# A graph-attention layer with residual and layer norm: rows led by their own column taken from SBUF instead of gathered

## The chip, the cores and the metric

The kernel runs on one core of one Trainium2 chip. The metric is the device time of one execution in microseconds (us). Before the change it was 237.32 us, the median of three runs (237.05 to 239.15).

Engine names are those of the profile: PE is TensorE (PEld its weight loads), DVE is VectorE, ACT is ScalarE, POOL is GpSimd, SP is the engine that issues most DMAs. A trailing q (SPq) stands for an engine's sequencer.

## The reference, cut to what matters

The inputs are x (4096 x 512), adj (4096 x 4096), W (512 x 2048, four heads of 512) and a (the attention vectors), all float32.

```
ht    = (x @ W) per head                                 # 4 heads, 4096 x 512
e     = leaky_relu(src[i] + dst[j], 0.01) + adj[i, j]    # src, dst: ht times a
att   = softmax(e over j)
h     = mean over heads of (att @ ht)
out   = layernorm(x + h)                                 # eps 1e-5, no gain
```

adj is not a mask here: its entries are 0 where there is no edge and otherwise random weights of up to 1e9, and the diagonal always has an edge. In a row whose largest entry stands far enough above the rest, the softmax puts all its weight on that one column c. Then h[i] = x[c] @ (mean of W over the heads), and the output row is layernorm(x[i] + x[c] @ W_mean).

## The kernel before, in words

`leading_rows` computes this short form for all rows and, beside it, a test that the leading entry is far enough ahead in every row. If a row fails the test, `general` computes its block in full; otherwise it is passed over.

**Tiling.** The 4096 rows are cut into NB = 32 blocks of 128. Partition p of block ib holds row p * 32 + ib. `hold` is one SBUF tile [128, 32, 512] for x of all blocks; at first its slots 16 to 31 hold W, and at the end each slot holds the block's output. `adj_t` has six buffers of 2 MB, one block each.

**The loop.** One step t of the loop (L408 on) works on several blocks at once:

- SP asks for four blocks of x where `x_at` says so (L403, L411), and for the adj tile of block t + 5 (L413). The first x load, for blocks 0 to 3, is asked for ahead of the loop (L132), behind the first five adj tiles and W.
- DVE reduces the adj tile of block t to the maxima of 64 segments of 64 columns, in two halves (`segment_maxima`, L163). Between the halves stands `find_column` of block t - 2 (L194): `max` and `max_index` in the 64 values of the leading segment, which a gather has fetched.
- POOL, for block t - 2, adds the segment's start to the place within the segment (L200) and gathers the 128 rows of x (`gather_rows`, L186) into `y`. In even steps it then computes the reciprocal deviation of two older blocks (`rstd`, L255 to L257).
- DVE finds the leading segment of block t (`find_segment`, L170 to L172). POOL turns it into a row of `adj_segs` (L174), gathers the segments (`lead`, L176), and multiplies the segment number by 64 (`start`, L181).
- PE, for block t - 3, transposes y (`turn`, L213; ACT copies the result, L215), adds the residual x by a product with the identity (`residual`, L221), and multiplies by the mean of W (`products`, L228). In the first steps it also transposes W and forms the vectors of the test (L334, L342).
- ACT takes the sums for the norm of block t - 4 (`stats`, L250, L252) and of x (`row_norm`, L235), and writes the finished blocks (`finish`, L261).

**Late blocks.** BEHIND is 24. For blocks 24 to 31 x is loaded only at the end; the products are put by and x is added later (`put_by`, `add_x`). The last block finds its column in the whole row (`find_column_in_row`). The stores follow the loop on SP (`store`, L313).

**What sets the order.** The kernel runs under a manual schedule: every engine executes its instructions in the order in which the Python code issues them. An engine that waits holds up all that is behind it in its own order. `small` tiles have five buffers each, `y` has four.

Of the kernel before, what the change touches and what calls it, by code (L numbers as in the profile page):

```python
# [9 lines left out]
F32 = mybir.dt.float32  # L10
U32 = mybir.dt.uint32
I32 = mybir.dt.int32
AF = mybir.ActivationFunctionType
OP = mybir.AluOpType
# [6 lines left out]
P = 128  # L21
C = 512
E = 64
# [3 lines left out]
def gat_resnorm_kernel(  # L27
# [29 lines left out]
    any_bad = keep.tile([1, 1], I32, name="any_bad")  # L57

    leading_rows(tc, x, adj, W, a, out, ident, v, n_bad, any_bad)

    flag = nc.values_load(any_bad[0:1, 0:1], min_val=0, max_val=N)
# [5 lines left out]
def leading_rows(ctx, tc, x, adj, W, a, out, ident, v, n_bad, any_bad):  # L67
# [8 lines left out]
    nc = tc.nc  # L76
    N, D = x.shape
    H = a.shape[0]
    KB, NB, S = D // P, N // P, N // E
    AHEAD = 5  # L80
    Q = 4
    PIECES = 4
    LATE = NB - Q
    BEHIND = LATE - Q

    once = ctx.enter_context(tc.tile_pool(name="once", bufs=1))
    adj_pool = ctx.enter_context(tc.tile_pool(name="adj_pool", bufs=AHEAD + 1))
    y_pool = ctx.enter_context(tc.tile_pool(name="y_pool", bufs=4))
    lead_pool = ctx.enter_context(tc.tile_pool(name="lead_pool", bufs=2 * Q + 1))
    small = ctx.enter_context(tc.tile_pool(name="small", bufs=5))  # L90
# [11 lines left out]
    hold = once.tile([P, NB, D], F32, name="hold")  # L102
# [1 line left out]
    w_sum = once.tile([P, KB, D], F32, name="w_sum")  # L104
    a_rows = once.tile([2 * H, D], F32, name="a_rows")

    once.tile([P, 32], F32, name="pad_end")
    adj_t = {}

    def pieces(ib):  # L110
# [30 lines left out]
    width = once.tile([P, 1], U32, name="width")  # L141
    nc.gpsimd.iota(width, pattern=[[0, 1]], base=E, channel_multiplier=0)
    power = once.tile([P, 2], F32, name="power")
    nc.gpsimd.memset(power, -0.5)
    eps = once.tile([P, 1], F32, name="eps")
    nc.gpsimd.memset(eps, EPS)

# [7 lines left out]
    seg_of, at_of, lead_of, y_t, yt_of, o_ps = {}, {}, {}, {}, {}, {}  # L155
# [12 lines left out]
    def find_segment(ib):  # L168
        seg = seg_of.pop(ib)
        nc.vector.max(out=top[:, ib, :], in_=seg)  # L170
        at = small.tile([P, 8], U32, name="at")
        nc.vector.max_index(at, top[:, ib, :], seg)  # L172
        row = small.tile([P, 1], U32, name="row")
        nc.gpsimd.tensor_tensor(row, at[:, 0:1], first[:, ib : ib + 1], op=OP.add)  # L174
        lead = lead_pool.tile([P, E], F32, name="lead")
        nc.gpsimd.indirect_dma_start(  # L176
            out=lead, out_offset=None, in_=adj_segs,
            in_offset=bass.IndirectOffsetOnAxis(ap=row[:, :1], axis=0),
        )
        start = at_of[ib] = small.tile([P, 1], U32, name="start")  # L180
        nc.gpsimd.tensor_tensor(start, at[:, 0:1], width, op=OP.mult)  # L181
        lead_of[ib] = lead

    def gather_rows(ib, col):
        y = y_t[ib] = y_pool.tile([P, D], F32, name="y")
        nc.gpsimd.indirect_dma_start(  # L186
            out=y, out_offset=None, in_=x,
            in_offset=bass.IndirectOffsetOnAxis(ap=col[:, :1], axis=0),
        )

    def find_inner(ib):
        nc.vector.max(out=inner[:, ib, :], in_=lead_of[ib])

    def find_column(ib):  # L194
        if ib < BEHIND:
            find_inner(ib)
        within = small.tile([P, 8], U32, name="within")
        nc.vector.max_index(within, top[:, ib, :], lead_of[ib])  # L198
        col = small.tile([P, 1], U32, name="col")
        nc.gpsimd.tensor_tensor(col, at_of.pop(ib), within[:, 0:1], op=OP.add)  # L200
        gather_rows(ib, col)

    def find_column_in_row(ib):

        col = small.tile([P, 8], U32, name="col")
        nc.vector.max_index(col, top[:, ib, :], adj_t[ib])
        gather_rows(ib, col)
# [192 lines left out]
        nc.vector.tensor_reduce(total, pg, axis=AX.X, op=OP.add)  # L400
        nc.vector.tensor_scalar(any_bad, total, -1.0, float(N), op0=OP.mult, op1=OP.add)

    x_at = {lo - 1: (lo, Q) for lo in range(Q, BEHIND, Q)}  # L403
    vectors = [(kb, h) for kb in range(KB) for h in range(H)]
    vectors_at = {t: 2 if t < 3 else 1 for t in range(1, 15)}
    COLUMN, PROJECT, STATS, FINISH = 2, 3, 4, 6
# [1 line left out]
    for t in range(NB):  # L408
# [7 lines left out]
        if t >= COLUMN:  # L416
            find_column(t - COLUMN)
# [4 lines left out]
        if t == NB - 1:  # L422
            for ib, n in ((BEHIND, 2), (LATE, Q), (BEHIND + 2, 2)):
                load_x(ib, n)
        find_segment(t)
        if t < 2:
            mean_of_heads(t)
# [8 lines left out]
        ib = t - PROJECT  # L436
# [23 lines left out]
    for ib in range(2 * Q, BEHIND, 2):  # L460
        store(nc.sync, ib, 2)
    find_column(NB - 2)
    add_x(nc.gpsimd, BEHIND)
    add_x(nc.gpsimd, BEHIND + 1)
# [211 lines left out]
```

## Time and profile before

| | |
|---|---|
| median of three runs | 237.32 us |
| span of the profiled execution | 235.7 us |
| DVE busy | 186.6 us (79%) |
| PE busy | 195.5 us (83%) |
| POOL busy | 100.9 us (43%) |
| ACT busy | 111.8 us (47%) |
| moved by DMA | 97.73 MB, mean 415 GB/s |
| gather of x rows (y), issue to landing, median | 7.7 us |
| gather of segments (lead), issue to landing, median | 6.1 us |
| adj tile of 2 MB, issue to landing, median | 31.8 us |

The profile is of one execution, whose span runs from its first to its last instruction; its time by the clock of the other runs isn't given apart from that, and the median stands 1.6 us above the span. A line of the timeline gives start and duration in us, engine, line of the kernel, operation, output tile and input tiles, with shapes, and in brackets how long the engine stood idle before it and what ended that. A line of a tile's view gives shortest/median/longest duration in ns, and the first and last start. The DMA row gives, for 40 equal slices of the span, the busy share in tenths (9 is 90% or more). A line of a queue gives packets, MB and the share of the 16 DMA engines' time.

### The profile page before, as it was taken

Reading aid. Unit: us, or ns where it says so; the run is one execution under the profiler, and the core shown is the slowest. Engines: PE = TensorE matmul, PEld = TensorE weight load, DVE = VectorE, ACT = ScalarE, POOL = GpSimd, SP = SyncE. Lnnn points to the kernel's source line nnn. Section 1 sums busy time; section 2 is a strip of 40 time slices with the busy share of each in tenths; the row PEclk is TensorE's granted clock in tenths of the full one; section 3 lists DMA queues with packets and bytes.
Section 4 is the critical chain, followed back from the end, with each engine's and each line's share of the span. In section 5 each row is a group of like instructions: output and inputs, shape, how many; then the busy total and the mean of one; then the engine's idle time right before and its main releaser. Section 6 shows DMA issues by size and latency. Waiting matters only on the chain.

```text
span 235.7 us, 2500 instructions
## 1 busy us (share of the span) xinstructions
PE 195.5 (83%) x683; PEld 100.9 (43%) x683; DVE 186.6 (79%) x302; ACT 111.8 (47%) x267; POOL 100.9 (43%) x215
## 2 busy tenths in 40 slices
PE   0198959999999899999969879688787987799991
PEld 0034526456555565665424333243333432245460
DVE  1735884589959995999589979998699899989772
ACT  2012012155757547474748355546464554137782
POOL 1112232415526462646353654464365564549130
PEclk9999799999999999999999999999997999999998
DMA  6999999999999999999999999999999999999995
GB/s 226 441 432 417 446 414 439 415 436 415 435 429 418 428 427 443 425 419 434 425 428 434 423 434 423 432 416 432 426 436 415 422 427 417 421 425 418 416 360 212
DMA packets 13697, 97.73 MB, mean 415 GB/s; under 512 B 2152, under 2 KB 2152, under 8 KB 7792
## 3 DMA queue, kind: packets, MB, share of 16 engines
q1 hardware_dynamic: 10080, 88.08, 88.5%
q0 software_dynamic: 3584, 9.44, 10.1%
q8 instruction: 6, 0.10, 0.2%
q14 instruction: 11, 0.09, 0.1%
q10 hardware_dynamic: 16, 0.02, 0.0%
HBM read 89.15 MB, written 8.39 MB: 414 GB/s over the span
## 4 chain that ended last, share of the span: by engine, by line
issue 33%; POOL 33%; DMA 18%; PE 9%; DVE 3%; POOLq 1%; ACT 1%; SPq 1%
DMA adj_t<-in_adj_dram 15%; POOL lead L176 11%; POOL y L186 10%; PE o L228 5%; POOL sd L256 4%; DMA y<-in_x_dram,col 3%; POOL start L181 2%; POOL col L200 2%; POOL row L174 2%; DVE seg L163 2%; PE o L270 2%; POOL sd L255 1%; POOL nm L257 1%; PE tp L213 1%; PE o L221 1%
## 5 line engine op out<-in xcount | busy, mean ns | idle before, releaser
L163 DVE TENSOR_REDUCE seg<-adj_t 128x32 f32<-128x2048 f32 (+1 forms) x68 | 145.9, 2150 | 35.3 <-DMA adj_t<-in_adj_dram 34.6
L228 PE MATMUL o<-w_sum,yt 128*128 128x512 f32 x248 | 116.5, 610 | 1.0 <-ACT yt L215 1.0
L228 PEld LDWEIGHTS o<-w_sum,yt 128*128 128x128 f32 x248 | 44.7, 193 | 54.9 <-issue 42.5
L215 ACT COPY yt<-tp 128x512 f32<-128x512 f32 x32 | 18.8, 588 | 47.3 <-PE tp L213 47.3
L176 POOL DMA_INDIRECT lead<-in_adj_dram,row x32 | 32.2, 1008 | 14.3 <-POOL row L174 14.3
L186 POOL DMA_INDIRECT y<-in_x_dram,col x32 | 30.8, 962 | 15.9 <-POOL col L200 15.6
L213 PE MATMUL tp<-ident,y 128*128 128x128 f32 x128 | 19.6, 276 | 15.0 <-DMA y<-in_x_dram,col 14.7
L318 PE MATMUL o<-hold,ident 128*128 128x512 f32 x32 | 18.6, 733 | 15.5 <-DMA hold<-in_L_gnn_W_dram 15.5
L221 PE MATMUL o<-hold,ident 128*128 128x512 f32 x52 | 26.9, 598 | 0.5 <-DMA hold<-in_x_dram 0.5
L213 PEld LDWEIGHTS tp<-ident,y 128*128 128x128 f32 x128 | 14.5, 141 | 28.2 <-issue 26.7
L200 POOL TENSOR_TENSOR col<-start,within 128x1 uint32<-128x1 uint32 x31 | 5.8, 188 | 45.7 <-DVE within L198 45.7
L336 ACT COPY wt<-tp 128x512 f32<-128x512 f32 x16 | 9.2, 587 | 32.4 <-PE tp L334 32.4
L174 POOL TENSOR_TENSOR row<-at,first 128x1 uint32<-128x1 uint32 x32 | 6.0, 188 | 39.3 <-DVE at L172 39.3
L235 ACT ACTIVATE sq<-hold 128x512 f32<-128x512 f32 x32 | 19.8, 620 | 0.0
L342 PEld LDWEIGHTS pv<-at_d,wt 128*128 128x128 f32 x128 | 16.3, 191 | 6.8 <-ACT wt L336 3.5
L318 PEld LDWEIGHTS o<-hold,ident 128*128 128x128 f32 x32 | 7.2, 237 | 24.6 <-POOL row L174 11.1
L319 ACT ACTIVATE w_sum<-o 128x512 f32<-128x512 f32 x4 | 2.4, 598 | 31.5 <-PE o L318 31.5
L261 ACT ACTIVATE hold<-o,nm,sd 128x512 f32<-128x512 f32 x24 | 17.2, 771 | 0.0
L252 ACT ACTIVATE sq<-o,nm 128x512 f32<-128x512 f32 x24 | 16.5, 687 | 0.8
L342 PE MATMUL pv<-at_d,wt 128*128 128x2 f32 x128 | 15.3, 244 | 0.6 <-ACT wt L336 0.6
L250 ACT ACTIVATE sq<-o 128x512 f32<-128x512 f32 x24 | 14.6, 607 | 0.0
L334 PEld LDWEIGHTS tp<-ident,hold 128*128 128x128 f32 x64 | 7.9, 142 | 6.9 <-issue 6.9
(85 smaller groups left out, 137.2 us busy)
## 6 DMA issues: line engine op xcount, KB each, us to landing
adj_t<-in_adj_dram SPq DMA_DIRECT2D x27, 2048.0 KB, 31.8
hold<-in_x_dram SPq DMA_DIRECT2D x7, 1024.0 KB, 32.6
adj_t<-in_adj_dram SPq DMA_DIRECT2D x6, 1024.0 KB, 28.3
out_dram<-hold SPq DMA_DIRECT2D x10, 512.0 KB, 15.0
adj_t<-in_adj_dram SPq DMA_DIRECT2D x8, 512.0 KB, 6.2
hold<-in_L_gnn_W_dram SPq DMA_DIRECT2D x4, 1024.0 KB, 17.3
out_dram<-hold SPq DMA_DIRECT2D x2, 1024.0 KB, 15.7
hold<-in_x_dram SPq DMA_DIRECT2D x2, 512.0 KB, 14.9
```

What stands on the lines that cost most here:

```text
L163: nc.vector.tensor_reduce(seg_of[ib][:, ts(k, S // n)], adj_t[ib][:, ts(k, N // n)].rearrange("p (s e) -> p s e", e=E), axis=AX.X, op=OP.max,)
L176: nc.gpsimd.indirect_dma_start(out=lead, out_offset=None, in_=adj_segs, in_offset=bass.IndirectOffsetOnAxis(ap=row[:, :1], axis=0),)
L186: nc.gpsimd.indirect_dma_start(out=y, out_offset=None, in_=x, in_offset=bass.IndirectOffsetOnAxis(ap=col[:, :1], axis=0),)
L213: nc.tensor.transpose(tp[:, kb, :], y[:, ts(kb, P)], ident)
L215: nc.scalar.copy(yt, tp)
L221: nc.tensor.matmul(o_ps[ib], ident, hold[:, ib, :], start=start, stop=False)
L228: nc.tensor.matmul(o_ps[ib], yt_of[ib][:, kb, :], w_sum[:, kb, :], start=(start and kb == 0), stop=(kb == KB - 1),)
L235: nc.scalar.activation(sq, hold[:, ib, :], AF.Square, accum_out=xx[:, ib : ib + 1])
L252: nc.scalar.activation(sq, o, AF.Square, bias=nm[:, i], accum_out=sd[:, i])
L261: nc.scalar.activation(hold[:, ib, :], o_ps.pop(ib), AF.Identity, bias=nm[:, i], scale=sd[:, i])
L318: nc.tensor.matmul(o, ident, hold[:, w_at + kb * H + h, :], start=(h == 0), stop=(h == H - 1))
L342: nc.tensor.matmul(pv[:, kb, h : 2 * H : H], wt[:, k, :], at_d[:, k, h : 2 * H : H], start=(k == 0), stop=(k == KB - 1),)
```

## The change

For blocks 0 to 23, rows whose leading column is their own row number are treated apart. The column is formed in float32 (`col_f`, from `start_f`, which replaces the integer `start`), compared with the row number (`own`, a new tile made by an iota), and 4096 is added to the index of the rows that are equal (`row_or_none`). y is first written by POOL as x of the block times the result of the comparison (`here`): x in the rows led by themselves, 0 elsewhere. Then the gather is issued with a bound of 4095, so that indices above it are passed over and those rows of y keep what POOL wrote. Blocks 24 to 31 keep the old path. The loads of x in the loop are asked for at step lo - 2 instead of lo - 1 for blocks lo to lo + 3. A padding tile is larger.

```diff
-    once.tile([P, 32], F32, name="pad_end")
+    once.tile([P, 128], F32, name="pad_end")
...
+    own = once.tile([P, NB], F32, name="own")
+    nc.gpsimd.iota(
+        own, pattern=[[1, NB]], base=0, channel_multiplier=NB, allow_small_or_imprecise_dtypes=True
+    )
...
-        start = at_of[ib] = small.tile([P, 1], U32, name="start")
-        nc.gpsimd.tensor_tensor(start, at[:, 0:1], width, op=OP.mult)
+        if ib < BEHIND:
+            start = small.tile([P, 1], F32, name="start_f")
+            nc.gpsimd.tensor_scalar(start, at[:, 0:1], float(E), None, op0=OP.mult)
+        else:
+            start = small.tile([P, 1], U32, name="start")
+            nc.gpsimd.tensor_tensor(start, at[:, 0:1], width, op=OP.mult)
+        at_of[ib] = start
...
+    def gather_others(ib, start, within):
+
+        col = small.tile([P, 1], F32, name="col_f")
+        nc.gpsimd.tensor_scalar(col, within, start, None, op0=OP.add)
+        here = small.tile([P, 1], F32, name="here")
+        nc.gpsimd.tensor_scalar(here, col, own[:, ib : ib + 1], None, op0=OP.is_equal)
+        row = small.tile([P, 1], U32, name="row_or_none")
+        nc.gpsimd.tensor_scalar(row, here, float(N), col, op0=OP.mult, op1=OP.add)
+        y = y_t[ib] = y_pool.tile([P, D], F32, name="y")
+        nc.gpsimd.tensor_scalar(y, hold[:, ib, :], here, None, op0=OP.mult)
+        nc.gpsimd.indirect_dma_start(
+            out=y, out_offset=None, in_=x,
+            in_offset=bass.IndirectOffsetOnAxis(ap=row[:, :1], axis=0),
+            bounds_check=N - 1, oob_is_err=False,
+        )
...
+        if ib < BEHIND:
+            gather_others(ib, at_of.pop(ib), within[:, 0:1])
+            return
...
-    x_at = {lo - 1: (lo, Q) for lo in range(Q, BEHIND, Q)}
+    x_at = {lo - 2: (lo, Q) for lo in range(Q, BEHIND, Q)}
```

## The prediction

> **What bounds the kernel now.** I read the page first (engine shares, DMA row, queues), then the engines' timelines around the waits, and last the chain.
>
> ```profile
> PE 195.5 (83%) x683; PEld 100.9 (43%) x683; DVE 186.6 (79%) x302; ACT 111.8 (47%) x267; POOL 100.9 (43%) x215
> DMA  6999999999999999999999999999999999999995
> q1 hardware_dynamic: 10080, 88.08, 88.5%
> q0 software_dynamic: 3584, 9.44, 10.1%
> ```
>
> The DMA row stands at nine tenths or more in 38 of 40 slices: the transfers are the resource with no slack, and no engine is full over the whole span. q0 carries POOL's gathers, 9.44 MB: 32 gathers of 128 x rows of 2 KB (8.39 MB) and 32 of 128 segments of 256 B. So bytes not gathered are DMA time, up to where something else takes over. VectorE's timeline tells where that is:
>
> ```profile
> 158.58 2.29 DVE L163 TENSOR_REDUCE seg<-adj_t 128x32 f32<-128x2048 f32 x1 [0.25 <-DMA adj_t<-in_adj_dram]
> 166.82 2.29 DVE L163 TENSOR_REDUCE seg<-adj_t 128x32 f32<-128x2048 f32 x1 [2.78 <-DMA adj_t<-in_adj_dram]
> 183.50 2.29 DVE L163 TENSOR_REDUCE seg<-adj_t 128x32 f32<-128x2048 f32 x1 [0.43 <-DMA adj_t<-in_adj_dram]
> 206.04 0.09 DVE L198 MATCH_VALUE_LOAD within<-top,lead 128x8 f32 x1 [0.39 <-DMA lead<-in_adj_dram,row]
> ```
>
> The bracket is idle time and its releaser. The wait at 166.8 (step 24) is the last long one for an adj tile; it comes once in four steps, behind each x load. From there VectorE runs its own steps back to back until the last tile is reduced at 209.7, then TensorE's chain of products runs to the last store. The end can move forward only as far as step 24 does. Steps are told by `within` (L198): done at 41.5 in step 4, 56.2 in 6, 105.8 in 14, 169.4 in 24, 180.2 in 26.
>
> Now POOL, over two steps:
>
> ```profile
> 103.77 0.96 POOL L176 DMA_INDIRECT lead<-in_adj_dram,row  x1 [0.51 <-POOL row L174]
> 104.75 0.20 POOL L181 TENSOR_TENSOR start<-at,width 128x1 uint32<-128x1 uint32 x1
> 105.91 0.19 POOL L200 TENSOR_TENSOR col<-start,within 128x1 uint32<-128x1 uint32 x1 [0.96 <-DVE within L198]
> 106.64 0.96 POOL L186 DMA_INDIRECT y<-in_x_dram,col  x1 [0.54 <-POOL col L200]
> 107.68 0.19 POOL L255 TENSOR_SCALAR sd<-sd 128x2 f32<-128x2 f32 x1
> 107.95 0.72 POOL L256 TENSOR_TENSOR sd<-sd,power 128x2 f32<-128x2 f32 x1
> 108.75 0.20 POOL L257 TENSOR_TENSOR nm<-nm,sd 128x2 f32<-128x2 f32 x1
> 108.90 0.19 POOL L174 TENSOR_TENSOR row<-at,first 128x1 uint32<-128x1 uint32 x1
> 109.47 1.06 POOL L176 DMA_INDIRECT lead<-in_adj_dram,row  x1 [0.38 <-POOL row L174]
> 110.57 0.21 POOL L181 TENSOR_TENSOR start<-at,width 128x1 uint32<-128x1 uint32 x1
> 111.49 0.19 POOL L200 TENSOR_TENSOR col<-start,within 128x1 uint32<-128x1 uint32 x1 [0.71 <-DVE within L198]
> ```
>
> POOL looks idle at 43%, but in an even step (with the three rstd operations) it waits only 0.7 us for VectorE. Without waits for other engines the even step costs it 4.9 us (105.91 to 110.78) and the odd one 3.6, together about 8.4, against 12.58 us for which two steps last (169.4 - 56.2, over nine pairs). It is in order: what is put ahead of the `lead` gather delays VectorE two steps later. Last, the start:
>
> ```profile
> 36.56 0.96 POOL L176 DMA_INDIRECT lead<-in_adj_dram,row  x1 [0.27 <-POOL row L174]
> 42.12 1.12 PE L221 MATMUL o<-hold,ident 128*128 128x512 f32 x2 [0.55 <-DMA hold<-in_x_dram]
> L244 POOL TENSOR_TENSOR hold<-hold,adj_t x3: 1273/1279/1283, 213.7 to 217.4; 128x512 f32<-128x512 f32 x3
> ```
>
> The first x load (blocks 0 to 3) lands only at 42.1, when TensorE waits for it, while POOL gathers y of block 0 already at 26.4. The last line is the only POOL operation on a 128x512 tile: 1.28 us with two inputs.
>
> **What the Trainium skill says.** GPSIMD Engine Reference, section "Elementwise — side-by-side cycle accounting": about 2.6 cycles an element at 1.2 GHz with two inputs (512 elements, 1.11 us, plus dispatch), and for a tight loop 769 ns measured on 512 elements. The trace agrees on the first (1.28 us); it shows nothing with one wide input. DMA: Bandwidth & Descriptors, section "Queues, rings and completion order": each DMA engine takes turns between the queues that have work, so gather bytes left out are turns for the adj stream. The trace fits: gathers land in 6.1 and 7.7 us while an adj tile needs 31.8. No page bears on what an index out of bounds costs.
>
> **The change, part by part.**
>
> *Rows skipped.* Counted in the reference's own inputs, 240 of the 3072 rows of blocks 0 to 23 have their maximum on the diagonal. 240 x 2048 B = 0.49 MB, at 427 GB/s (the rate of the middle windows) 1.15 us. Only the 204 rows of blocks 0 to 20 are gathered in time to move the tile of step 24: 0.98 us. That is the ceiling of the gain at the end.
>
> *Small operations.* `col` (0.19) becomes col_f, here and row_or_none, three dependent ones of 0.27 each start to start (as L255 to L256), and start_f stands for start. Unshown: whether compare and scalar forms cost more; L255, a TENSOR_SCALAR, costs 0.19, so I take that.
>
> *The wide multiply* y = hold x here. Unshown. Below: ident's TENSOR_SCALAR_AFFINE_SELECT on 128x128 took 0.29 us, so four times the width at least 0.5. Above: 1.28 us (L244). I take 0.8, the skill's 512-element price. The gather then waits 0.54 us for y as it did for col. So `within` to y gather grows from 0.73 to 0.81 + 0.80 + 0.54 = 2.15 us, +1.42 per block, bounds +1.1 to +1.9; 24 blocks are 34 us of POOL. The check of bounds I take at nothing, with 0 to 0.25 us per gather kept for the range.
>
> *What that does to the cadence.* Every even step's `lead` needs the one two steps before. The loop: 0.08 handshake, 2.15, y gather 1.04, rstd 1.23, row 0.57, landing of lead 6.1, `within` 0.5: 11.7 us. POOL itself needs 5.0 + 6.25 = 11.25 for both steps. Until step 14 TensorE's turns of W hold a pair at 12.12 (turns at 97.65, 103.71, 109.77). All are under 12.58, so the addition hides under the DMA stream, with under 1 us to spare per pair.
>
> *The new wait for x.* Block 0's multiply reads hold and waits for the first x load; behind it in POOL's queue stand y of block 0, lead of 2, y of 1, lead of 3. These four, 0.59 MB, no longer precede the load, so it lands 1.4 us sooner, at 40.7. Then multiply to 41.5, y gather 42.0, row 43.1, lead of block 2 43.6 (was 29.2), landed 49.7, `within` in step 4 at 50.2 instead of 41.5: VectorE is 8.7 us late, TensorE's first block likewise. Does DMA run dry? No: four to five adj tiles are in flight (31.8 us from issue to landing). Recovery: steps 5 and 6 go at VectorE's own 5.55, 11.1 where they took 14.7: 5.0 late at step 6. Four pairs to step 14 at 12.12 against 12.41 (105.8 - 56.2): 3.8 late. Five pairs to step 24 at 11.7 (58.5) against 63.6 give back 5.1: all made up, by little, so step 24 is DMA-bound again, 0.9 sooner. From 24 to 26 VectorE took 10.8; the loop needs 11.7 less 0.2 (no L192), so `within` comes at 168.5 + 11.5 = 180.0 against 180.2. After that blocks take the old path.
>
> *x two steps ahead.* The bytes stay; each x load passes one adj load on SP, so the gap behind it comes a step earlier (7, 11, ... 23). It lands one step before its multiply. SP waits no longer for it: nothing. The larger pad and `own`: nothing; one more iota at the start hides before 10.5, when POOL first has work.
>
> *Sum:* -0.2 us against the profiled span, 235.5 for 235.7; the median of the runs, 237.32, has 1.6 us around that, taken as unchanged: 237.1.
>
> **The rivals.**
> *POOL paces the loop (slower).* If multiply plus check cost 1.28 us, POOL needs 5.5 + 6.7 = 12.2 for two steps: the delay of 5.4 at step 6 shrinks by only 9 x 0.37 = 3.3, and steps 24 to 26 take 12.2 instead of 10.8: +3.3, 240.6. At 1.5 us it is 12.65, nothing is recovered: +8, 245. It decides from about 1.05 us. For it: 1.28 is the only wide POOL row, and the descriptor work with bounds isn't shown; against: one input, not two.
> *The skip moves no bytes less* (an index out of bounds still takes its turn): the recovery still holds, the ceiling is gone: +0.5, 237.8. Against it only that a row not written must not be fetched.
> *Cheap POOL (0.5 us):* the loop is 11.4 and the end takes most of the ceiling: -0.8, 236.5; I count it with the forecast.
>
> **The numbers.** A measurement of this kernel tells about 1% (2.4 us) from no change. Forecast with the cheap case 0.60; POOL pacing 0.27, nearly all over +1%; no bytes saved 0.08; 0.05 for what I don't see, mostly a gain over the ceiling. Low end 235.9: ceiling plus 0.3% noise; high end 241.5: pacing at 1.33 us, which leaves out 0.11 above and 0.04 below.
>
> **What would show it.** POOL's busy time rising from 101 to about 135 us; the multiply near 0.8 us; y of block 0 gathered near 42 instead of 26; `within` waiting for lead in steps 4 to 6; q0 at about 8.95 MB; a wait for an adj tile at step 23 still there, near 161. If that wait is gone and `within` waits for lead in most even steps, POOL paces. If POOL's first multiply starts near 27, the first x load isn't the wait I take it for. It is all wrong if y's landing, not lead's, turns out to hold the steps.

## The result, and the profile after

The changed kernel takes 255.32 us, the median of four runs (254.58 to 257.74), against 238.02 for the kernel before in the runs beside it. The ratio is 1.074, with an interval of 1.066 to 1.081: 17 us slower. The profiled execution has a span of 252.9 us, 17.2 more than before.

The page of the changed kernel, its engine shares, the DMA row and the queue of the gathers:

```profile
PE 201.0 (79%) x683; PEld 103.8 (41%) x683; DVE 186.4 (74%) x302; ACT 112.1 (44%) x267; POOL 159.9 (63%) x288
DMA  6999999999999999999999999999999999972215
q0 software_dynamic: 3584, 8.95, 9.4%
```

The change does what it says: q0 moved 8.95 MB for 9.44. But POOL is busy for 59 us more, and DMA, full to the end before, has little to do in the last four slices. The loads run ahead and the engines come behind. Who waits for whom (columns: total us, times, longest), first the kernel before, then the changed one:

```profile
DVE seg L163 <- DMA adj_t<-in_adj_dram: 34.6, 14, 5.5
DVE within L198 <- DMA lead<-in_adj_dram,row: 1.0, 2, 0.6
```

```profile
DVE inner L217 <- DMA lead<-in_adj_dram,row: 33.6, 17, 10.9
POOL row L178 <- DVE at L176: 22.5, 6, 8.6
DVE seg L167 <- DMA adj_t<-in_adj_dram: 16.9, 6, 5.5
POOL y L209 <- DMA hold<-in_x_dram: 13.5, 1, 13.5
```

VectorE used to wait for adj tiles, now it waits for the `lead` gathers. Its last wait for an adj tile is at 38.2; before it was at 183.5. The sum of VectorE's work is unchanged (186.4 us).

POOL over two steps of the changed kernel, from its timeline:

```profile
100.29 0.29 POOL L203 TENSOR_SCALAR col_f<-within,start_f 128x1 f32<-128x1 uint32 x1
100.68 0.29 POOL L205 TENSOR_SCALAR here<-col_f,own 128x1 f32<-128x1 f32 x1
101.08 0.27 POOL L207 TENSOR_SCALAR row_or_none<-here,col_f 128x1 uint32<-128x1 f32 x1
101.45 1.58 POOL L209 TENSOR_SCALAR y<-hold,here 128x512 f32<-128x512 f32 x1
103.31 1.11 POOL L210 DMA_INDIRECT y<-in_x_dram,row_or_none  x1 [0.28 <-POOL y L209]
...
106.15 0.30 POOL L203 TENSOR_SCALAR col_f<-within,start_f 128x1 f32<-128x1 uint32 x1
...
113.48 0.29 POOL L203 TENSOR_SCALAR col_f<-within,start_f 128x1 f32<-128x1 uint32 x1
```

POOL waits for no other engine here, in the lines left out neither. The two steps last 13.19 us (100.29 to 113.48), all of it POOL's own work and the gaps between its dependent operations. Before, two steps lasted 12.58 on the mean of nine pairs; in the changed kernel the same nine pairs last 13.31. From the first operation to the start of the y gather it is 3.02 us instead of 0.73.

The end of `within` (L198 before, L223 in the changed kernel) in some steps, in us of each profiled execution, and how far the changed kernel is behind:

| step | before | changed | behind |
|---|---|---|---|
| 4 | 41.5 | 51.8 | 10.3 |
| 6 | 56.2 | 65.2 | 9.0 |
| 14 | 105.8 | 118.9 | 13.1 |
| 24 | 169.4 | 185.0 | 15.5 |
| 28 | 191.2 | 209.7 | 18.5 |
| last (block 30) | 211.3 | 228.9 | 17.6 |

So the loss has two parts: some 9 us at the start, and a slower pace that adds 6.5 from step 6 to 24. Two or three more come between steps 24 and 28, where VectorE waits for `lead` three times, 3.2 us in all, while POOL works off blocks 22 and 23.

### The profile page after: what moved, and what is told of

The parts are those of the page before. It is cut to its first block, busy times and chain, and to the rows that moved or that the text cites. A ratio compares the mean times of both kernels' runs of the same rounds, so it can differ in the third digit from the quotient of the medians.

```text
span 252.9 us, 2596 instructions
## 1 busy us (share of the span) xinstructions
PE 201.0 (79%) x683; PEld 103.8 (41%) x683; DVE 186.4 (74%) x302; ACT 112.1 (44%) x267; POOL 159.9 (63%) x288
## 3 DMA queue, kind: packets, MB, share of 16 engines
q0 software_dynamic: 3584, 8.95, 9.4%
## 4 chain that ended last, share of the span: by engine, by line
POOL 42%; DMA 21%; issue 17%; PE 16%; DVE 2%; ACT 1%; POOLq 0%
POOL y L209 12%; PE o L256 9%; DMA adj_t<-in_adj_dram 9%; POOL y L210 8%; POOL lead L180 8%; DMA lead<-in_adj_dram,row 6%; DMA y<-in_x_dram,row_or_none 3%; POOL sd L284 3%; DMA y<-in_x_dram,col 3%; POOL here L205 2%; POOL col_f L203 2%; PE o L249 2%; PE tp L241 2%; POOL row L178 2%; POOL start_f L186 1%
## 5 line engine op out<-in xcount | busy, mean ns | idle before, releaser
L256 PE MATMUL o<-w_sum,yt 128*128 128x512 f32 x248 | 117.7, 616 | 1.0 <-ACT yt L243 1.0
L256 PEld LDWEIGHTS o<-w_sum,yt 128*128 128x128 f32 x248 | 45.5, 195 | 56.1 <-issue 43.7
L209 POOL TENSOR_SCALAR y<-hold,here 128x512 f32<-128x512 f32 x24 | 38.0, 1582 | 15.6 <-DMA hold<-in_x_dram 13.5
L241 PE MATMUL tp<-ident,y 128*128 128x128 f32 x128 | 20.6, 286 | 29.1 <-DMA y<-in_x_dram,row_or_none 25.8
L346 PE MATMUL o<-hold,ident 128*128 128x512 f32 x32 | 19.4, 761 | 15.9 <-DMA hold<-in_L_gnn_W_dram 15.9
L217 DVE MAX8 inner<-lead 128x8 f32<-128x64 f32 x32 | 6.5, 221 | 33.7 <-DMA lead<-in_adj_dram,row 33.6
L210 POOL DMA_INDIRECT y<-in_x_dram,row_or_none x24 | 26.6, 1106 | 6.7 <-POOL y L209 6.7
L249 PE MATMUL o<-hold,ident 128*128 128x512 f32 x52 | 28.4, 630 | 0.0
L370 PEld LDWEIGHTS pv<-at_d,wt 128*128 128x128 f32 x128 | 17.2, 200 | 7.4 <-issue 4.1
L289 ACT ACTIVATE hold<-o,nm,sd 128x512 f32<-128x512 f32 x24 | 17.2, 771 | 0.0
L370 PE MATMUL pv<-at_d,wt 128*128 128x2 f32 x128 | 16.0, 249 | 0.6 <-ACT wt L364 0.6
```

Source lines behind the costliest of these rows:

```text
L209: nc.gpsimd.tensor_scalar(y, hold[:, ib, :], here, None, op0=OP.mult)
L210: nc.gpsimd.indirect_dma_start(out=y, out_offset=None, in_=x, in_offset=bass.IndirectOffsetOnAxis(ap=row[:, :1], axis=0), bounds_check=N - ...
L241: nc.tensor.transpose(tp[:, kb, :], y[:, ts(kb, P)], ident)
L249: nc.tensor.matmul(o_ps[ib], ident, hold[:, ib, :], start=start, stop=False)
L256: nc.tensor.matmul(o_ps[ib], yt_of[ib][:, kb, :], w_sum[:, kb, :], start=(start and kb == 0), stop=(kb == KB - 1),)
L289: nc.scalar.activation(hold[:, ib, :], o_ps.pop(ib), AF.Identity, bias=nm[:, i], scale=sd[:, i])
```

## The experiments

Two theories stood against each other at first: POOL's pace makes the loss by itself, or the stall at the start is a loss of its own. A third suspect was the order of the loads. Ratios are to runs of the kernel before on the same chip, with the 95% interval.

### The x loads alone

```diff
 # the kernel before
-    x_at = {lo - 1: (lo, Q) for lo in range(Q, BEHIND, Q)}
+    x_at = {lo - 2: (lo, Q) for lo in range(Q, BEHIND, Q)}
```

> The kernel before with one part of the change alone: the x loads of the loop asked for at step lo - 2 instead of lo - 1. Theory (POOL's added work and its wait for the first x load make the 17 us): same as before, 238 us within 1 us, waits for an adj tile move from steps 8, 12, ... to 7, 11, ... Rival (the order of the loads matters by itself, x passing an adj tile delays VectorE): 2 us or more slower than before.

Measured: 237.16 us, ratio 0.999 (0.9965 to 1.001). `within` is 2.9 to 3.0 us behind in steps 7, 11 and 15 and 0.5 or less in the step after each. VectorE's wait moves by one step, as expected, and costs nothing. The order of the loads by itself is out.

### Pace without stall

```diff
 # the changed kernel, at both places
-        if ib < BEHIND:
+        if Q <= ib < BEHIND:
```

> The changed kernel, with blocks 0 to 3 on the old path (gathered in full, no multiply), so that POOL never waits for the first x load. Theory (the stall of 13.5 us at the start costs about 9 us, and POOL's pair of steps of 13.2 us never pays it back): about 246 us, within 2; within of step 6 within 1 us of before, POOL still full from about step 8 on. Rival (POOL's pace alone makes the whole loss, the stall is hidden behind it as a slack that would be used up anyway): 252 us or more.

Measured: 247.55 us, ratio 1.038 (1.030 to 1.046), as expected. Step 6 is 1.1 us behind the kernel before, step 24 8.4, step 28 10.7; the nine pairs of steps between 6 and 24 last 13.4 us on the mean. (The profiled execution was 1.4 us behind already at step 2, before anything of the change acts, and so was that of the next run.) The slower pace alone costs about 10 us, and it costs it with no stall ahead.

### Stall without pace

```diff
 # the changed kernel, at both places
-        if ib < BEHIND:
+        if ib < Q:
```

> The new path for blocks 0 to 3 alone, the old one for 4 to 23: the stall of POOL at the start stays, the slower pace goes. Theory (stall and pace only cost together: with the old pace of 8.4 us of POOL for two steps the delay of some 9 us at step 6 is paid back by step 24 out of the 14 us in which VectorE waits for adj tiles): within 1 us of before. Rival (a stall at the start is a loss of its own that stays): 243 us or more.

Measured: 240.94 us, ratio 1.012 (1.006 to 1.018), between the two expectations. Step 6 is 10.3 us behind, step 24 3.5, the end 2 to 4. The delay is paid back for two thirds, not in full: a pair lasted 11.8 us. Two waits of the trace stand in the way. POOL's rstd waits for ScalarE's sums, which come behind TensorE, and behind step 16 VectorE waits 2.46 us for a product of the test, which also comes late from TensorE (0.56 us in the kernel before):

```profile
105.40 0.19 POOL L283 TENSOR_SCALAR sd<-sd 128x2 f32<-128x2 f32 x1 [1.84 <-ACT sq L280]
117.52 0.19 POOL L283 TENSOR_SCALAR sd<-sd 128x2 f32<-128x2 f32 x1 [2.25 <-ACT sq L280]
131.59 0.19 DVE L382 TENSOR_REDUCE n<-px 128x8 f32<-128x32 f32 x1 [2.46 <-PE px L380]
```

How much each of the two waits costs was not tried apart.

The profiled spans are longer by 4.1 us with the stall alone, by 10.2 with the pace alone, by 17.2 with both. The two together cost about 3 us more than their sum (3.7 by the medians, 3.6, 10.0 and 17.3). That fits a POOL that is full, so that the stall has nothing from which to be paid back. Neither of the two theories was right alone.

### The wide operation left out

```diff
 # blocks 0 to 3 on the old path, and
-        nc.gpsimd.tensor_scalar(y, hold[:, ib, :], here, None, op0=OP.mult)
```

> Blocks 0 to 3 on the old path, and the multiply left out in the others: the rows led by themselves are skipped by the gather and y keeps an older block's row there, so this part of the computation is missing. No engine writes y but the gather. Theory (the multiply of 1.58 us, not the small operations or the gather with bounds, makes POOL the pace, and the run with ScalarE failed because the copy stood at the end of ScalarE's step): POOL's pair falls from 13.2 to about 9.5 us, 236.5 to 238 us. Rival (the longer way from within to the gather costs by itself): 240 us or more.

Measured: 236.94 us, ratio 0.998 (0.995 to 1.001). POOL waits for VectorE again, and VectorE hardly for `lead`:

```profile
POOL col_f L203 <- DVE within L222: 16.5, 20, 2.0
DVE inner L216 <- DMA lead<-in_adj_dram,row: 3.9, 5, 0.9
```

The small operations and the gather with bounds are still there (0.29, 0.29, 0.27 and 1.12 us). So with them in place and without the stall, the wide operation makes the whole difference to the run with the slower pace, 247.55 us; a run with it and without the small operations was not made. Step 24 ends 0.8 us ahead of before; from step 26 on that is gone, with VectorE waiting 0.6 and 0.7 us for `lead` in steps 25 and 26.

### Half the width

```diff
 # the changed kernel
-        nc.gpsimd.tensor_scalar(y, hold[:, ib, :], here, None, op0=OP.mult)
+        n = D if ib < Q else D // 2
+        nc.gpsimd.tensor_scalar(y[:, :n], hold[:, ib, :n], here, None, op0=OP.mult)
```

> The changed kernel with the multiply on half of the columns in blocks 4 to 23 (in the other half the rows led by themselves keep older values: that part is left out). The wide operation should take about 0.9 us, near the 0.8 of the prediction. By the prediction's recurrence: the early delay is paid back, 237.5 to 239 us. By the corrected one (small operations 0.40 apart instead of 0.27, gather 1.10 instead of 0.96, so a loop of 12.3 us for two steps against 12.58): only some 3 of 9 us are paid back by step 24, 243 to 246 us.

Measured: 247.94 us, ratio 1.047 (1.042 to 1.051). The operation took 0.94 us, close to the price of the prediction, and still nothing was paid back: 8.8 us behind at step 6, 10.2 at step 24. A pair lasted 12.7 us, more than both recurrences gave, and both expectations missed. So even near the price that I had assumed, the step "all made up" fails.

POOL's own work for two steps was at most 12.2 us (103.5 to 115.7), so something else is longest. The trace shows hardly any landing times, but a wait of VectorE for `lead` ends with the landing. In five of the six odd steps from 13 to 23 it waited, and there `lead` had been issued 7.4 to 9.2 us before. For block 13:

```profile
114.22 0.97 POOL L180 DMA_INDIRECT lead<-in_adj_dram,row  x1 [0.28 <-POOL row L178]
122.90 0.23 DVE L218 MAX8 inner<-lead 128x8 f32<-128x64 f32 x1 [2.25 <-DMA lead<-in_adj_dram,row]
```

From the end of `within` in step 13 (110.1) to that in step 15 (123.3) it is 13.2 us: 4.1 to the issue of `lead`, 8.7 to its landing, 0.4 for VectorE. The way through `lead` in the odd steps, which the prediction's recurrence doesn't contain, is the longest here. It is read from the trace; no run changes it alone.

### All rows fetched

```diff
 # the changed kernel
-        nc.gpsimd.tensor_scalar(row, here, float(N), col, op0=OP.mult, op1=OP.add)
+        nc.gpsimd.tensor_scalar(row, here, 0.0, col, op0=OP.mult, op1=OP.add)
```

> The changed kernel, but the index of a row led by itself stays its own column, inside the bound: the same POOL work, all rows fetched. Theory (bytes are not what sets the time any more): within 1 us of the changed kernel, about 255 us, q0 back at 9.44 MB, gather on POOL still 1.10 us. Rival (an index out of bounds costs POOL or the queue something): 1 us or more faster than the changed kernel, gather back at 0.96 us.

Measured: 254.64 us, ratio 1.076 (1.073 to 1.079), q0 at 9.44 MB. The 0.49 MB are worth nothing that can be measured where POOL sets the pace. The gather with bounds took 1.10 us here too, with no index outside: passing rows over costs POOL nothing measurable; against the 0.96 us of the old gather the form with bounds is 0.14 longer.

### What the operation costs in four forms

```diff
 # the changed kernel
-        nc.gpsimd.tensor_scalar(y, hold[:, ib, :], here, None, op0=OP.mult)
+        h = hold[:, ib, :]
+        if ib % 4 == 0:
+            nc.gpsimd.tensor_scalar(y, h, here, None, op0=OP.mult)
+        elif ib % 4 == 1:
+            nc.gpsimd.tensor_copy(y, h)
+        elif ib % 4 == 2:
+            nc.gpsimd.tensor_scalar(y, h, 1.0, None, op0=OP.mult)
+        else:
+            nc.gpsimd.tensor_tensor(y, h, here.to_broadcast([P, D]), op=OP.mult)
```

> The changed kernel, where y is written in four ways by block number modulo 4: times the column here (0), a plain copy (1), times the constant 1.0 (2), times here spread over the row as a second wide operand (3). In all four the output is the same, as the gather overwrites the other rows. It measures the operation: if the column as scalar operand makes the 1.58 us, copy and constant take 0.8 us or less and the two-operand form 1.28; if any TENSOR_SCALAR of this width is slow on POOL, 0 and 2 agree at 1.6 and only the copy is less.

The view of tile y in this run (shortest/median/longest ns, first and last start, form):

```profile
L211 POOL TENSOR_SCALAR y<-hold,here x6: 1578/1580/1584, 41.0 to 171.9; 128x512 f32<-128x512 f32 x6
L213 POOL COPY y<-hold x6: 611/611/612, 46.8 to 179.2; 128x512 f32<-128x512 f32 x6
L215 POOL TENSOR_SCALAR y<-hold x6: 1510/1515/1517, 53.3 to 184.2; 128x512 f32<-128x512 f32 x6
L217 POOL TENSOR_TENSOR y<-hold,here x6: 1041/1042/1042, 59.2 to 191.4; 128x512 f32<-128x512 f32 x6
```

At this width the dear form is the TENSOR_SCALAR, with a column or with a constant, and neither the copy nor the form with a second operand: the copy takes 0.61 us, and the product with two operands, expected at 1.28, takes 1.04. The durations of each form vary by less than 0.01 us over the blocks, so no slowing by what runs beside them shows. The one run of this kernel gave 250.74 us.

### Copies in its place

The factor `here` isn't needed, since the gather overwrites the other rows. So a copy can stand for the multiply; three places were tried. The first is ScalarE, where the multiply stood:

```diff
 # the changed kernel
-        nc.gpsimd.tensor_scalar(y, hold[:, ib, :], here, None, op0=OP.mult)
+        nc.scalar.copy(y, hold[:, ib, :])
```

> The changed kernel with the wide multiply on POOL replaced by a copy of the block's x into y on ScalarE (the gather overwrites the other rows, so the factor isn't needed). The wait for the first x load stays, now on ScalarE and through y on POOL. Theory (the wide operation of 1.58 us is what makes POOL the pace): a pair of steps needs 13.2 - 3.2 = 10 us of POOL, the early delay of about 10 us shrinks by more than half by step 24, total 238 to 242 us. Rival (descriptor work with bounds and the three small operations are enough to hold the pace): 248 us or more.

Measured: 261.56 us, ratio 1.096 (1.087 to 1.104), slower than the change itself. With blocks 0 to 3 on the old path besides:

> Both edits: copy on ScalarE, and blocks 0 to 3 on the old path. Theory: neither stall nor pace is left, what remains are 0.4 MB fewer bytes: 237 to 238.5 us, not slower than before. Rival (something else of the change costs, such as the longer way from within to the y gather, which TensorE waits for): 240 us or more.

Measured: 255.10 us, ratio 1.071 (1.064 to 1.079). Both theories missed. By the number the rivals came about (248 and 240 us or more), but not by their mechanism. The timeline of the second shows it (the bracket is idle time and its releaser):

```profile
150.28 0.62 ACT L263 ACTIVATE sq<-hold 128x512 f32<-128x512 f32 x1
150.89 1.43 ACT L289 ACTIVATE hold<-o,nm,sd 128x512 f32<-128x512 f32 x2
152.21 0.62 ACT L209 COPY y<-hold 128x512 f32<-128x512 f32 x1
153.61 1.12 POOL L210 DMA_INDIRECT y<-in_x_dram,row_or_none  x1 [3.55 <-ACT y L209]
```

In ScalarE's order the copy stands behind all of the step before, down to `finish`. Here that step began only when TensorE had transposed: ScalarE stood idle for 5.27 us until 148.39. POOL waited for the copy 17 times, 39.7 us in all. The edit replaced a long operation by a long wait.

Next POOL's plain copy, and last ScalarE's copy one step ahead, behind the copy of the transposed block (with x asked for at lo - 3), both with blocks 0 to 3 on the old path:

```diff
+        nc.gpsimd.tensor_copy(y, hold[:, ib, :])            # the one: in place of the multiply
...
+    def own_rows(ib):                                       # the other
+        y = y_t[ib] = y_pool.tile([P, D], F32, name="y")
+        nc.scalar.copy(y, hold[:, ib, :])
...
             turn(ib)
+            if Q <= t - 1 < BEHIND:
+                own_rows(t - 1)
```

> Blocks 0 to 3 on the old path, and in the others POOL's plain copy (0.61 us on this tile) in place of the multiply (1.58 us). The output is whole. Theory (lead lands about 1.2 us behind the y gather that stands ahead of it in the queue, whatever else POOL does; two steps need 0.1 + 2.1 to the y gather + 8.1 landing + 1.2 + 0.5 = 12.0 us, POOL itself 11.2, against 12.58): 237 to 239 us. Rival (the room is used up, delays add as in the run with half the columns): 241 us or more.

> Blocks 0 to 3 on the old path; y of the other blocks is filled by a copy on ScalarE one step ahead, behind its copy of the transposed block, so that neither engine waits for it; x asked for three steps ahead. The output is whole. Theory: like the run without any wide operation, 236.5 to 237.5 us, at best 1 us under before, with 0.4 MB fewer bytes. Rival (ScalarE's 0.6 us per step or a wait for x stands in TensorE's way): 238.5 us or more.

Measured: 237.86 us, ratio 1.001 (0.998 to 1.004), and 238.07 us, ratio 1.001 (0.999 to 1.004). Both take back the whole loss, and neither gains; the first was expected so, the second at 236.5 to 237.5. No version beats the kernel before by what can be measured.

### The lead gather ahead of the y gather

Landings in the kernel before and in the changed one showed `lead` mostly 1.2 us behind the y gather issued ahead of it. Whether that is the cause was tried on the kernel before:

```diff
-        gather_rows(ib, col)
+        col_of[ib] = col
...
         find_segment(t)
+        if t >= COLUMN:
+            gather_rows(t - COLUMN, col_of.pop(t - COLUMN))
```

> The kernel before, with each step's y gather issued on POOL behind the step's lead gather instead of ahead of it. Theory (lead lands about 1.2 us behind the y gather that stands just ahead of it in the same queue, so its landing of 6.1 us is mostly y's): lead lands in 5 us or less from its issue. Rival (a gather needs about 6 us beside the adj stream whatever stands ahead of it): lead still lands in about 6 us. The time of the whole is expected at 238 to 241 us: y comes some 2 us later to TensorE.

Measured: 261.44 us, ratio 1.094 (1.085 to 1.104). Between 90 and 170 us of its span, where six landings of `lead` are in the trace, two took 5.8 and 5.9 us with over 3.6 us between `lead` and the y gather before it, and four took 7.8 or 7.9 where that gather was issued 1.6 us earlier. Under 5 us was not seen there. So my theory was right only for a gather close behind another; the rival holds for the rest. Closeness isn't all of it: at 182.5, also 1.6 us behind a y gather, `lead` landed in 5.7, and why isn't known. The time was a surprise, and the waits say why:

```profile
POOL sd L257 <- ACT sq L254: 63.3, 14, 7.0
```

A y gather now starts 4.9 us behind `col` (140.2 to 145.1) instead of 0.7. TensorE waits 31.6 us for y in all, for 14.7 before, ScalarE comes later with it, rstd on POOL waits for ScalarE's sums (5.6 us before), and behind rstd stand the next `lead` and y.

## Why the prediction was wrong, by its own steps

**The sign and the rival.** The rival "POOL paces the loop" came about, and beyond its own bounds. I gave it 0.27 and 240.6 to 245 us; it was 255.32. Its sign came too: no wait for an adj tile after 38.2, and VectorE waiting for `lead` in 7 of the 11 even steps from 4 to 24 (and in 9 of the 10 odd ones).

**The wide multiply** is the step that failed first. I took 0.8 us, from the price of a tight loop in the Trainium skill (GPSIMD Engine Reference, section "Elementwise — side-by-side cycle accounting", 769 ns for 512 elements); it measured 1.58. The page calls that the best case of such a loop and ties it to no operation. With 1.58 alone, my own sum of 11.25 us for POOL's two steps becomes 12.8, above the 12.58 under which it was to hide; with the bound's 0.14, counted as the rival counts it, it is 13.1, close to the 13.2 measured. I took L244 with its two inputs, 1.28 us, for the upper bound; that reasoning, fewer inputs and so not longer, is refuted: TENSOR_SCALAR with one wide input is slower than TENSOR_TENSOR with two. From half width (0.94) to full it is 2.5 ns an element. The copy, 0.61 us, stays under the skill's price.

**The small operations** were taken as 0.27 apart; they are 0.39, 0.40 and 0.37. The wait of the gather for y, taken as 0.54, is 0.28. Together with the multiply the way from `within` to the y gather grew by 2.29 us per block, not 1.42, above the upper bound of 1.9. The gather itself took 1.10 us, 0.14 more, inside my 0 to 0.25. POOL's busy time rose to 160 us, not 135.

**The stall at the start** was right in place, and in size to 1.6 us. The multiply of block 0 began at 40.75 (predicted 40.7), `lead` of block 2 was issued at 44.2 (43.6) and landed in 7.2 us (6.1), and `within` of step 4 ended at 51.8 (50.2).

**The recovery** is the other step that failed. VectorE didn't run steps 5 and 6 at its own 5.55 us: it waited for `lead` in step 5, and step 6 was 9.0 us late instead of 5.0. At 13.3 us a pair the delay grew where it should have shrunk. The error isn't only the size of the multiply: at 0.94 us nothing was paid back either, and with the old pace (the stall alone) 3.5 us were left at step 24. My recurrence followed `lead` through the even steps alone and let it land in 6.1 us. In the odd steps no rstd stands between the gathers, so `lead` is issued 1.6 us behind y: of the nine such gathers for blocks 5 to 21 in the changed kernel eight landed in 7.3 to 8.2 us, those for the even blocks 6 to 20 in 5.8 to 7.4. (For blocks 22 to 25, odd and even, it was 5.3 to 5.7; why isn't known.) And the recovery has no wait for TensorE or ScalarE in it after step 14, while in the run with the stall alone both came late (2.46 us for the product of the test, 1.8 and 2.3 us for ScalarE's sums).

**The ceiling.** Up to 0.98 us at step 24 fits: 0.8 ahead there where no wide operation stood in the way, with 0.42 of the 0.49 MB saved; it is one profiled execution, and with POOL's copy step 24 was 0.4 behind. That the loop would take it back between 24 and 26 fits too, at 0.2 left predicted and none seen. (The low end of the range, ceiling plus 0.3%, is 235.6 by these terms, not 235.9; nothing hangs on it.)

**x two steps ahead** costing nothing was right, by its own run.

## What to carry to other kernels

The busy share of an engine doesn't say what it has to spare: here one at 43% had no room for 2.3 us a step. Count its work and its gaps over one period of the loop and hold that against the period before putting anything on it, and follow every way round the loop, the odd steps as well as the even. Price an operation by its own form; a bound from another form of the same width isn't one. A saving of 0.5% of the bytes didn't pay here even for a copy of 0.61 us on the path that feeds the stream, and a delay at the start was paid back only as far as the engines in the loop had room.

## What the runs showed of the hardware that I had not expected

On a 128x512 float32 tile in SBUF, GpSimd took 0.61 us for a copy, 1.04 for a product with a column spread over the row as second operand, 1.28 for a sum of two wide tiles, 1.51 for a product with a constant and 1.58 for a product with a column given as scalar. A gather of x rows took POOL 0.96 us without a bound; with one it took 1.10 us in the changed kernel, the same where no index was outside, and up to 1.14 in the other runs. So both forms of TENSOR_SCALAR took longer than both of TENSOR_TENSOR. A `lead` gather of 128 segments of 256 B, beside the full stream of adj, landed mostly in 7.3 to 8.2 us when a y gather of 128 rows had been issued 1.6 us before it, up to block 21 of the changed kernel.
